# Storing each 1 MiB output tile as two 64-partition transfers in a pairwise-product kernel

## The chip, the cores and the metric

The kernel runs on one core of a Trainium2 chip. The metric is the device time of one execution in microseconds (us). Before the change it is 766.14 us, the median of three runs that lie between 765.97 and 767.21 us. The profiled execution has a span of 769.8 us, from its first to its last instruction.

## What is computed

The inputs are 1024 samples of 32 fields, each a vector of 128 numbers, and one 128x128 matrix for each of the 496 pairs of fields (i, j) with i < j. Everything is float32.

```python
v_i = inputs[:, I_IDX, :]                        # 1024 x 496 x 128
v_j = inputs[:, J_IDX, :]
transformed = jnp.einsum('bpd,ped->bpe', v_i, W) # one 128x128 matrix per pair
return transformed * v_j                         # 1024 x 496 x 128
```

The output is 1024 x 496 x 128 float32 numbers, 260 MB. The two inputs together are some 49 MB.

## The kernel before

**Layout.** The 128 embedding entries lie on the 128 partitions. A field is a tile `x_f` of 128 partitions x 1024 samples, and all 32 fields stay resident after their load. The host transposes the inputs before and the output after; in device memory the output is laid out as `(248, 128, 2, 1024)`: for each group of two pairs, 128 rows of 2 x 1024 numbers. So one row of one group is 8192 contiguous bytes, and one group is a contiguous block of 1 MiB.

**Loops.** The main loop goes over units `u`: unit `2q + h` is pair `q` and half `h` of the samples (512 of them, `HB`). `first(u)` does the matmuls for a unit into a PSUM tile `po` (L154 for the first 15 pairs in plain float32; L157 for the other pairs, with a matrix split in two parts, and L158 scales the result on ScalarE). `second(u)`, three units later (`LAG`), adds a third matmul (L166) and multiplies the result by field `j` on VectorE (L172), writing into the output tile `ot`. An `ot` tile holds one group, that is two pairs of 1024 samples on 128 partitions (1 MiB), and is filled by four multiplications. The pool has four `ot` tiles, so a fifth group can be started only when the store of the first has landed. ScalarE (L94, L109) and GpSimd (L95 to L97, L110 to L115) split matrices and fields into high and low parts ahead of their use; VectorE does some of the last subtractions (L195).

**Transfers.** The matrices come in 124 blocks of four pairs, a load of 256 KiB each (L85), 16 pairs ahead; the fields come in loads of 512 KiB (L76), five fields ahead. The group's store is issued when its fourth multiplication is queued (L176). All stores and, but for the four first field loads, all loads are issued from the same queue, that of SyncE (SP), in the order of the program[...]. The last group is stored in four pieces (L174), one for each half of each pair. Each transfer raises one of eight semaphores, taken in turn.

Of the kernel before, what the change touches and what calls it, by code (L numbers as in the profile page):

```python
# [1 line left out]

# [4 lines left out]

F32 = mybir.dt.float32
F32R = mybir.dt.float32r
ALU = mybir.AluOpType  # L10

P = 128
NF = 32
NQ = NF * (NF - 1) // 2
BT = 1024
HB = 512
WC = 2
WL = 4
OG = 2
EPS = 2.0**-12  # L20
NATIVE = 5
SHARED = 10
XDLAG = 10
LAG = 3
WLEAD = 4
XLEAD = 5


def _pairs():

    return [(i, j) for i in range(NF - 2, -1, -1) for j in range(i + 1, NF)]


@with_exitstack
def kernel(
    ctx: ExitStack,
    tc: tile.TileContext,
    xt: bass.AP,
    wt: bass.AP,
    out: bass.AP,  # L40
):

    nc = tc.nc
    pairs = _pairs()
    nchunk = NQ // WC  # L60

    xpool = ctx.enter_context(tc.tile_pool(name="x", bufs=1))
    spool = ctx.enter_context(tc.tile_pool(name="xs", bufs=2))
    rpool = ctx.enter_context(tc.tile_pool(name="wr", bufs=5))
    wpool = ctx.enter_context(tc.tile_pool(name="ws", bufs=4))
    opool = ctx.enter_context(tc.tile_pool(name="o", bufs=4))
    ppool = ctx.enter_context(tc.tile_pool(name="ps", bufs=8, space=bass.MemoryType.PSUM))

    x_sb = {}

    def load_x(f, n=1, pieces=1, eng=None):

        t = xpool.tile([P, n, BT], F32, tag=f"x{f}", name=f"x_{f}")
        s = BT // pieces
        for k in range(pieces):
            (eng or nc.sync).dma_start(out=t[:, :, k * s : (k + 1) * s], in_=xt[:, f : f + n, k * s : (k + 1) * s])  # L76
        for k in range(n):
            x_sb[f + k] = t[:, k, :]

    w_raw = {}  # L80

    def load_w(c, splits=(0, WL)):
        w_raw[c] = rpool.tile([P, WL, P], F32, tag="w", name=f"w_{c}")
        for a, b in zip(splits, splits[1:]):
            nc.sync.dma_start(out=w_raw[c][:, a:b, :], in_=wt[c, :, a:b, :])  # L85

    w_s = {}

    def split_w(c, u):

        k = c * WC % WL
        raw = w_raw[c * WC // WL][:, k : k + WC, :].rearrange("p q e -> p (q e)")
        h, l, d = [wpool.tile([P, WC * P], F32R, tag=t, name=f"{t}_{c}") for t in ("wh", "wl", "wd")]
        nc.scalar.mul(h, raw, 1.0 - 2.0**-13)  # L94
        nc.gpsimd.tensor_tensor(l, raw, h.bitcast(F32), ALU.subtract)  # L95
        nc.gpsimd.tensor_scalar(d, h.bitcast(F32), EPS, 1.0, ALU.mult, ALU.mult)  # L96
        nc.gpsimd.tensor_tensor(d, l.bitcast(F32), d.bitcast(F32), ALU.subtract)  # L97
        w_s[c] = (h, l, d)

    x_s = {}  # L100
    later = []

    def split_x(f, a, u):

        if a == 0:
            x_s[f] = [spool.tile([P, BT], F32R, tag=t, name=f"{t}_{f}") for t in ("xh", "xl", "xd")]
        s = slice(a, a + HB)
        h, l, d = [t[:, s] for t in x_s[f]]
        nc.scalar.mul(h, x_sb[f][:, s], 1.0 - 2.0**-13)  # L109
        nc.gpsimd.tensor_tensor(l, x_sb[f][:, s], h.bitcast(F32), ALU.subtract)  # L110
        nc.gpsimd.tensor_scalar(l, l.bitcast(F32), 1.0 / EPS, 1.0, ALU.mult, ALU.mult)  # L111
        if f > NF - 2 - NATIVE - SHARED:
            later.append((min(u + XDLAG, 2 * first_q[f] + LAG - 1), d, h.bitcast(F32), l.bitcast(F32)))
        else:
            nc.gpsimd.tensor_tensor(d, h.bitcast(F32), l.bitcast(F32), ALU.subtract)  # L115

    nq0 = NATIVE * (NATIVE + 1) // 2
    c0 = nq0 // WC
    first_q = {i: q for q, (i, j) in reversed(list(enumerate(pairs)))}

    todo = []
    for c in range(c0, nchunk):
        todo.append(((c - 3) * WC + 1, max(c * WC, nq0), lambda u, c=c: split_w(c, u)))
    for i in range(NF - 2 - NATIVE, -1, -1):
        for a in range(0, BT, HB):
            todo.append((first_q[i + 1] + 1 if i < NF - 3 - NATIVE else 2, first_q[i], lambda u, i=i, a=a: split_x(i, a, u)))
    todo.sort(key=lambda t: t[1])

    load_w(0, (0, 1, WL))
    load_x(NF - 2, pieces=2, eng=nc.scalar)
    load_x(NF - 1, pieces=2, eng=nc.scalar)
    load_x(NF - 3)
    load_x(NF - 4)
    load_w(1)
    for f in range(NF - 5, NF - 4 - XLEAD, -1):
        load_x(f)
    load_w(2)
    load_w(3)  # L140


    ctx.enter_context(tc.manual_schedule())
    po, ots = {}, {}


    def first(u):
        q, h = divmod(u, 2)
        i, c = pairs[q][0], q // WC
        r = slice(q % WC * P, (q % WC + 1) * P)  # L150
        s = slice(h * HB, (h + 1) * HB)
        po[u] = ppool.tile([P, HB], F32, tag="po", name=f"po_{u}")
        if q < nq0:
            nc.tensor.matmul(po[u], w_raw[q // WL][:, q % WL, :], x_sb[i][:, s], start=True, stop=True)  # L154
        else:
            for t in (0, 1):
                nc.tensor.matmul(po[u], w_s[c][t][:, r], x_s[i][t][:, s], start=t == 0, stop=t == 1)  # L157
            nc.scalar.mul(po[u], po[u], 1.0 + EPS)  # L158

    def second(u):  # L160
        q, h = divmod(u, 2)
        i, j = pairs[q]
        r = slice(q % WC * P, (q % WC + 1) * P)
        s = slice(h * HB, (h + 1) * HB)
        if q >= nq0:
            nc.tensor.matmul(  # L166
                po[u], w_s[q // WC][2][:, r], x_s[i][2][:, s], start=False, stop=True, skip_group_check=True
            )
        g, k = divmod(q, OG)
        if k == 0 and h == 0:  # L170
            ots[g] = opool.tile([P, OG, BT], F32, tag="ot", name=f"ot_{g}")
        nc.vector.tensor_tensor(ots[g][:, k, s], po.pop(u), x_sb[j][:, s], ALU.mult)  # L172
        if q >= NQ - 2:
            nc.sync.dma_start(out=out[g, :, k, s], in_=ots[g][:, k, s])  # L174
        elif k == OG - 1 and h == 1:
            nc.sync.dma_start(out=out[g], in_=ots[g])  # L176

    for u in range(2 * NQ + LAG):
        q = u // 2
        if u % (2 * WL) == 0 and (q // WL + WLEAD) * WL < NQ:  # L180
            load_w(q // WL + WLEAD)
        if u < 2 * NQ:
            i, j = pairs[q]
            if u % 2 == 0 and j == i + 1 and 0 <= i - 2 - XLEAD:
                load_x(i - 2 - XLEAD)
            first(u)
        if u >= LAG:
            second(u - LAG)
        if u % 2 == 1:
            ready = [t for t in todo if t[0] <= q]  # L190
            if ready:
                ready[0][2](u)
                todo.remove(ready[0])
        while later and later[0][0] <= u:
            nc.vector.tensor_tensor(*later.pop(0)[1:], ALU.subtract)  # L195
    assert not todo and not later


# [25 lines left out]
```

## Time and profile before

| what | value |
|---|---|
| time, median of 3 runs | 766.14 us (765.97 to 767.21) |
| span of the profiled execution | 769.8 us |
| busy: TensorE matmul, VectorE, ScalarE, GpSimd | 722.7, 632.0, 638.7, 593.2 us |
| bytes moved by the DMA engines | 310.11 MB, mean 403 GB/s |
| written to device memory, read from it | 260.05 MB, 49.28 MB |
| granted TensorE clock | 0.994 of full speed |

The bytes and their rate say what the 16 DMA engines of the core did over the whole span. The busy time of a compute engine is a sum over its instructions; an engine may be busy all the time and still not set the end, so the chain of waits has to be read beside it.

### The profile page before, as it was taken

How to read it: one execution, taken by the hardware profiler on the slowest of the kernel's cores; microseconds unless marked ns; L12 is line 12 of the kernel's file. 1: busy time of each engine (PE TensorE's matmuls, PEld its weight loads, DVE VectorE, ACT ScalarE, POOL GpSimd, SP SyncE). 2: the span in 40 equal slices, each digit the busy share in tenths (PEclk: the TensorE clock that was granted, in tenths of full speed). 3: DMA queues.
4: the chain of work that ended last, by engine and by line, in shares of the span. 5: the costliest groups of instructions: out<-in, count | busy, mean ns of one | idle time of the engine just before them, and what ended most of it. 6: DMA issues, size and time to landing. Idle time of an engine off the chain costs nothing.

```text
span 769.8 us, 11824 instructions
## 1 busy us (share of the span) xinstructions
PE 722.7 (94%) x2946; PEld 545.4 (71%) x2946; DVE 632.0 (82%) x1012; ACT 638.7 (83%) x1256; POOL 593.2 (77%) x863
## 2 busy tenths in 40 slices
PE   7988999999999999999999989999999999999994
PEld 3556766677777676777777767777777777777773
DVE  4869888888888788888888878888888888888885
ACT  2276988888888898888888889998988898998983
POOL 2677998887889878878878696978786969697660
PEclk9999999999999999999999999999999999999998
DMA  9999999999999999999999999999999999999997
GB/s 352 424 419 384 407 397 410 405 400 406 410 405 403 400 409 416 409 379 421 411 414 407 412 403 406 411 407 408 415 410 395 408 410 409 409 408 405 400 401 307
DMA packets 59108, 310.11 MB, mean 403 GB/s; under 512 B 6560, under 2 KB 6816, under 8 KB 27424
## 3 DMA queue, kind: packets, MB, share of 16 engines
q1 hardware_dynamic: 58464, 308.31, 99.4%
q10 hardware_dynamic: 576, 1.05, 0.4%
q8 instruction: 24, 0.39, 0.2%
q14 instruction: 44, 0.36, 0.1%
HBM read 49.28 MB, written 260.05 MB: 402 GB/s over the span
## 4 chain that ended last, share of the span: by engine, by line
DMA 61%; DVE 21%; PE 15%; issue 2%; DVEq 0%; SPq 0%; ACT 0%
DMA out_dram<-ot 60%; DVE ot L172 19%; PE po L157 9%; PE po L166 4%; DVE xd L195 2%; PE po L154 1%; DMA x<-in_xt_dram 1%; DVEq L172 0%; SPq L85 0%; DVEq L217 0%; ACT po L158 0%; DVEq L195 0%
## 5 line engine op out<-in xcount | busy, mean ns | idle before, releaser
L172 DVE TENSOR_TENSOR ot<-po,x 128x512 f32<-128x512 f32 x992 | 618.6, 684 | 129.5 <-DMA out_dram<-ot 70.2
L158 ACT ACTIVATE po<-po 128x512 f32<-128x512 f32 x962 | 551.2, 583 | 106.5 <-PE po L157 53.3
L157 PE MATMUL po<-xh,wh 128*128 128x512 f32 x962 | 388.7, 404 | 24.4 <-DVE ot L172 21.6
L166 PE MATMUL po<-xd,wd 128*128 128x512 f32 x962 | 376.9, 392 | 5.7 <-DVE xd L195 5.7
L157 PE MATMUL po<-xl,wl 128*128 128x512 f32 x962 | 377.6, 392 | 2.2 <-POOL wl L95 2.1
L157 PEld LDWEIGHTS po<-xh,wh 128*128 128x128 f32 x962 | 180.9, 188 | 110.2 <-DVE ot L172 72.5
L95 POOL TENSOR_TENSOR wl<-w,wh 128x256 fp32r<-128x256 f32 x241 | 179.2, 744 | 92.1 <-ACT wh L94 90.7
L166 PEld LDWEIGHTS po<-xd,wd 128*128 128x128 f32 x962 | 181.0, 188 | 46.3 <-ACT po L158 3.8
L157 PEld LDWEIGHTS po<-xl,wl 128*128 128x128 f32 x962 | 181.1, 188 | 36.8 <-POOL wl L95 4.5
L97 POOL TENSOR_TENSOR wd<-wl,wd 128x256 fp32r<-128x256 f32 x241 | 180.0, 747 | 20.1
L96 POOL TENSOR_SCALAR wd<-wh 128x256 fp32r<-128x256 f32 x241 | 99.1, 411 | 20.3
L94 ACT ACTIVATE wh<-w 128x256 fp32r<-128x256 f32 x241 | 99.2, 412 | 0.5 <-DMA w<-in_wt_dram 0.5
L110 POOL TENSOR_TENSOR xl<-x,xh 128x512 fp32r<-128x512 f32 x52 | 67.3, 1293 | 19.8 <-ACT xh L109 19.5
L115 POOL TENSOR_TENSOR xd<-xh,xl 128x512 fp32r<-128x512 f32 x32 | 41.4, 1292 | 2.7
L109 ACT ACTIVATE xh<-x 128x512 fp32r<-128x512 f32 x52 | 32.5, 628 | 10.5 <-DMA x<-in_xt_dram 10.3
L111 POOL TENSOR_SCALAR xl<-xl 128x512 fp32r<-128x512 f32 x52 | 32.8, 631 | 4.6
L154 PE MATMUL po<-x,w 128*128 128x512 f32 x60 | 29.0, 645 | 4.1 <-DMA x<-in_xt_dram 4.1
L154 PEld LDWEIGHTS po<-x,w 128*128 128x128 f32 x60 | 12.1, 206 | 20.2 <-issue 13.9
L195 DVE TENSOR_TENSOR xd<-xh,xl 128x512 fp32r<-128x512 f32 x20 | 16.6, 831 | 0.0
L109 ACT ACT_TABLE_LOAD x1 | 1.3, 1283 | 2.6 <-issue 2.6
L211 POOL MEMSET const-float32-0.0<- 128x1 f32 x1 | 0.1, 98 | 0.2 <-issue 0.2
L211 POOL MEMSET const-bfloat16-1.0<- 128x1 bf16 x1 | 0.1, 101 | 0.0
(2 smaller groups left out, 0.2 us busy)
## 6 DMA issues: line engine op xcount, KB each, us to landing
out_dram<-ot SPq DMA_DIRECT2D x247, 1024.0 KB, 8.9
w<-in_wt_dram SPq DMA_DIRECT2D x123, 256.0 KB, 9.1
x<-in_xt_dram SPq DMA_DIRECT2D x30, 512.0 KB, 9.5
x<-in_xt_dram ACTq DMA_DIRECT2D x4, 256.0 KB, 5.1
out_dram<-ot SPq DMA_DIRECT2D x4, 256.0 KB, 7.0
w<-in_wt_dram SPq DMA_DIRECT2D x1, 192.0 KB, 3.6
w<-in_wt_dram SPq DMA_DIRECT2D x1, 64.0 KB, 2.9
```

The source lines that it names most:

```text
L94: nc.scalar.mul(h, raw, 1.0 - 2.0**-13)
L95: nc.gpsimd.tensor_tensor(l, raw, h.bitcast(F32), ALU.subtract)
L96: nc.gpsimd.tensor_scalar(d, h.bitcast(F32), EPS, 1.0, ALU.mult, ALU.mult)
L97: nc.gpsimd.tensor_tensor(d, l.bitcast(F32), d.bitcast(F32), ALU.subtract)
L109: nc.scalar.mul(h, x_sb[f][:, s], 1.0 - 2.0**-13)
L110: nc.gpsimd.tensor_tensor(l, x_sb[f][:, s], h.bitcast(F32), ALU.subtract)
L115: nc.gpsimd.tensor_tensor(d, h.bitcast(F32), l.bitcast(F32), ALU.subtract)
L154: nc.tensor.matmul(po[u], w_raw[q // WL][:, q % WL, :], x_sb[i][:, s], start=True, stop=True)
L157: nc.tensor.matmul(po[u], w_s[c][t][:, r], x_s[i][t][:, s], start=t == 0, stop=t == 1)
L158: nc.scalar.mul(po[u], po[u], 1.0 + EPS)
L166: nc.tensor.matmul(po[u], w_s[q // WC][2][:, r], x_s[i][2][:, s], start=False, stop=True, skip_group_check=True)
L172: nc.vector.tensor_tensor(ots[g][:, k, s], po.pop(u), x_sb[j][:, s], ALU.mult)
```

## The change

The store of a group, one transfer of 128 partitions, becomes two transfers of 64 partitions each, issued one behind the other from the same queue: first partitions 0 to 63, then 64 to 127. The bytes, their place in memory, the length of the rows (8192 bytes) and the condition for issuing (the group's four multiplications) stay as they are. It is for changing which partitions each of the 16 DMA engines reads: a transfer's rows are shared out among the engines[...]. The four small stores of the last group are not touched.

```diff
         elif k == OG - 1 and h == 1:
-            nc.sync.dma_start(out=out[g], in_=ots[g])
+            for a in range(0, P, P // 2):
+                nc.sync.dma_start(out=out[g, a : a + P // 2], in_=ots[g][a : a + P // 2])
```

## Prediction

> **What bounds the kernel now.** I read the page's slices and DMA part first, since the kernel writes 260 MB; then the chain that ended last; then one stretch of it in order of time; then the waits of the issuing queue. The page:
>
> ```profile
> DMA  9999999999999999999999999999999999999997
> DMA packets 59108, 310.11 MB, mean 403 GB/s; under 512 B 6560, under 2 KB 6816, under 8 KB 27424
> q1 hardware_dynamic: 58464, 308.31, 99.4%
> HBM read 49.28 MB, written 260.05 MB: 402 GB/s over the span
> DMA 61%; DVE 21%; PE 15%; issue 2%; DVEq 0%; SPq 0%; ACT 0%
> out_dram<-ot SPq DMA_DIRECT2D x247, 1024.0 KB, 8.9
> w<-in_wt_dram SPq DMA_DIRECT2D x123, 256.0 KB, 9.1
> ```
>
> The 16 DMA engines have packets in every slice, and one queue's packets fill 99.4% of what 16 engines have. A store takes 8.9 us from issue to landing, and a load a quarter of its size takes 9.1 us: neither moves for that long, both stand in line. The busy time by stretches says the same for the steady part:
>
> ```profile
> core 0: us, PE busy (x) PEld busy (x) DVE busy (x) ACT busy (x) POOL busy (x), PEclk, DMA share, GB/s
> 540.00:640.00 100.00, 98.40 (x413) 75.96 (x412) 85.46 (x138) 90.69 (x179) 78.80 (x117) 1.00 1.01 407
> ```
>
> DMA share 1.01 at 407 GB/s: the engines never rest, 407 / 16 = 25.4 GB/s each. TensorE shows 98% too, but the chain decides:
>
> ```profile
> 23 pieces in order of time: start us, us, what
> 635.72 8.91 DMA out_dram<-ot
> ...
> 644.76 2.50 DVE ot L172 x4
> ...
> 647.27 8.98 DMA out_dram<-ot
> ...
> 656.37 2.50 DVE ot L172 x4
> ...
> 658.88 8.93 DMA out_dram<-ot
> ```
>
> The chain is a ring: a store lands, VectorE fills the freed tile (2.50 us), its store lands 8.9 us later. One turn is 647.27 - 635.72 = 11.55 us and covers four groups, as there are four `ot` tiles: 2.89 us a group. In a turn the queue moves four stores (4.19 MB) and two matrix loads (0.52 MB), 4.72 MB / 11.55 us = 408 GB/s, the rate above. So the ring's period is the DMA engines' throughput; the 8.9 us is queueing behind other stores. By bytes, a store has 11.55 x 4 / 4.5 / 4 = 2.57 us of it, a matrix load 0.64 us.
>
> The issuing queue has room:
>
> ```profile
> SPq L176 <- DVE ot L172: 481.8, 244, 4.4
> ```
>
> (who waits for whom on it: us in total, times, longest), and by the tile's view
>
> ```profile
> L176 SPq DMA_DIRECT2D out_dram<-ot x247: 332/332/1258, 14.3 to 759.0; - x124
> ```
>
> It stands 481.8 us waiting for VectorE; an issue costs 332 ns.
>
> [...] Here each of the 128-partition transfers raises its semaphore by 16 single steps. [...]
>
> **The change part by part.**
>
> Descriptors: each of 247 stores has a second completion write on each engine. The trace's packet records give 9 ns for one: 247 x 0.009 = 2.2 us, on the path, as the engines never rest.
>
> Issue: 247 more issues of 332 ns are 82 us of the queue, beside its 481.8 us of waiting: hidden. Behind the second issue stands at most a matrix or field load, 0.33 us later; loads run 16 pairs ahead (eight groups, 23 us), so nobody waits. Eight semaphores taken in turn may make an issue wait for the eighth transfer before it. Per group there are now 2 halves + 0.5 load = 2.5 transfers (1.5 before), so eight are 3.2 groups; today 8.9 / 2.89 = 3.1 groups are in flight. The engines keep about the same amount queued: 0.
>
> Engine work: the same 64 KiB per engine and store. If each engine still gave 25.4 GB/s, nothing else would change.
>
> Ports: this is the term that counts. Each engine takes four rows (32 KiB) of the lower half, then four of the upper. [...] By half of today's 407 GB/s it takes 5.15 us, +2.57. [...]
>
> They are not fully in step. [...] From the semaphore steps in the trace: of the 16 engines of a transfer, twelve finish within 0.69 us (median), the others 1.9 to 4.7 us after the first. Two of the twelve are thus some 0.3 us apart (my choice within 0 to 0.69), while a half takes 2.57 / 2 = 1.29 us. Sharing then holds for (1.29 - 0.3) / 1.29 = 77%[...].
>
> The compute engines, faster than this, wait: VectorE's four multiplications (4 x 0.68 = 2.7 us a group) lie within 4 us or more of storing.
>
> **The rivals.**
>
> *Ports do not bind, or the engines fall into opposite halves.* [...] Also, the trace before cannot tell whether 25.4 GB/s is the engine's or the port's limit. Then only the completion writes count: 766.1 + 2.2 = 768.3 us, slower by 0.3%. [...]
>
> *Slow packets vanish (faster).* The mean packet is 11 ns over the median; if the new sharing-out spreads the addresses so that all are gone, 8 x 247 x 0.011 = 22 us is saved, less 2.2: 746 us. If a quarter goes, 763 us. For it: the chain is DMA throughput, so it would count in full. Against it: nothing ties the slow packets to partitions[...].
>
> *The queue's semaphores become the wait.* If issues waited for older transfers so that only two groups were in flight, the ring would be two groups in about 2.5 (fill) + 5.8 us (two groups' transfers of 2.89), 4.1 us a group, near 1030 us. Worked out above, 3.2 groups stay possible; I give it little.
>
> **How the numbers follow.** Ports shared, mostly in step to half in step (about 940 to 1340 us): 0.74. Ports shared but engines well apart, or the semaphore wait alone (770 to 940): 0.05. No port effect, completion writes only (around 768): 0.08, half of it within 0.2%. Faster: 0.13. So faster 0.13, within 0.2% 0.04, slower 0.83. The predicted time is that of the likeliest case, 1190 us. The upper end takes in [...]some of the 5.15 us price: 1340. The first case alone holds less than 8 in 10, so the lower end reaches down to the completion-write case, 768 us.
>
> **What would show it.** Right: the share of the DMA engines stays near 1 while GB/s falls to about 260 (310 MB / 1.19 ms); 8192-byte packets go from 309 ns to some 500 to 610; a half's time to landing exceeds 8.9 us clearly; TensorE and VectorE fall to about 60 and 53% busy with the same busy time per instruction; the chain goes nearly all to the DMA; VectorE's wait for the store, 70.2 us in total now, grows to several hundred. Wrong: packets still at 309 ns and 400 GB/s, which means that the ports do not bind; or packets at 309 ns with gaps between them (DMA share below 0.9), which means a wait for issue or semaphores. [...]

## The result and the profile after

The changed kernel takes 1034.24 us (median of four runs, 1027.89 to 1039.99) against 766.67 us (four runs, 765.97 to 773.16), 1.347 times the time before, with a 95% interval of 1.339 to 1.356. The profiled execution has a span of 1033.4 us.

The page of the changed kernel: DMA totals, the main queue, the chain by engine, VectorE's multiplications (busy, mean ns | idle before, releaser) and the median us from issue to landing.

```profile
DMA packets 63064, 310.16 MB, mean 300 GB/s; under 512 B 10512, under 2 KB 10768, under 8 KB 31376
q1 hardware_dynamic: 62416, 308.32, 94.7%
DMA 67%; DVE 18%; PE 7%; SPq 4%; issue 2%; DVEq 1%; POOL 0%; ACT 0%; POOLq 0%
L172 DVE TENSOR_TENSOR ot<-po,x 128x512 f32<-128x512 f32 x992 | 619.8, 684 | 388.6 <-DMA out_dram<-ot 312.9
out_dram<-ot SPq DMA_DIRECT2D x494, 512.0 KB, 6.6
w<-in_wt_dram SPq DMA_DIRECT2D x123, 256.0 KB, 5.8
```

The bytes are the same to 0.05 MB, the rate falls from 403 to 300 GB/s, and the packet count grows by 247 x 16 = 3952 packets of 4 bytes, the completion writes (6561 before, 10513 after, 8.9 ns each), and four packets of other queues. A multiplication still takes 684 ns; VectorE now waits 312.9 us for stores (70.2 before). So the loss lies in the transfers. But a half lands in 6.6 us (a whole store before: 8.9) and a load in 5.8 (9.1): the line in front of each transfer is shorter than before, not longer. The stretch shown before, again:

```profile
core 0: us, PE busy (x) PEld busy (x) DVE busy (x) ACT busy (x) POOL busy (x), PEclk, DMA share, GB/s
540.00:640.00 100.00, 73.83 (x288) 53.15 (x287) 59.55 (x96) 64.62 (x125) 56.81 (x84) 0.98 0.95 294
```

The engines are at work for 0.95 of the time (1.01 before) and move 294 GB/s (407): their packets have become slower, and some 5% of the time they have none. Both can be read from the packet records. Per engine (sums over all packets, divided by 16), packets took 770.4 us before and 984.3 us after: 8192-byte ones +184.2 us (mean 320 to 413 ns), 2048-byte ones +18.7, 4096-byte ones +8.7, completion writes +2.3. The span is longer than their sum by 1033.4 - 984.3 = 49.1 us, by nothing before. 184.2 + 18.7 + 8.7 + 2.3 + 49.1 = 263 us is the whole difference of the two spans, 263.6 us.

Where the second part comes from shows in the issuing queue. The timeline of SyncE, the kernel before first (start us, us, then what; xN joins N neighbours):

```profile
start us, us, engine line op out<-in xcount [idle before <-releaser]
606.78 2.91 SPq L176 DMA_DIRECT2D out_dram<-ot  x2
609.79 0.73 SPq L85 DMA_DIRECT2D w<-in_wt_dram  x1
612.61 2.88 SPq L176 DMA_DIRECT2D out_dram<-ot  x2
615.58 0.79 SPq L85 DMA_DIRECT2D w<-in_wt_dram  x1
```

and the changed kernel:

```profile
start us, us, engine line op out<-in xcount [idle before <-releaser]
605.84 6.08 SPq L177 DMA_DIRECT2D out_dram<-ot  x4
612.02 1.53 SPq L85 DMA_DIRECT2D w<-in_wt_dram  x1
613.64 6.52 SPq L177 DMA_DIRECT2D out_dram<-ot  x4
620.25 1.54 SPq L85 DMA_DIRECT2D w<-in_wt_dram  x1
```

The pieces before have pauses within them: two issues of 0.33 us in 2.9 us. After, four issues fill 6.1 to 6.5 us without one. The output tile's view gives one issue (ns, min/median/max), before it was 332/332/1258:

```profile
L177 SPq DMA_DIRECT2D out_dram<-ot x494: 466/1631/2746, 14.0 to 1023.6; - x165
```

This price isn't all due to the form of the transfer. An issue that began less than 0.15 us after the end of the one in front of it was long before the change too. There these were mostly the matrix loads, whose issues stand right behind a store's. They too are transfers of 128 partitions; the view of their tile, before the change:

```profile
L85 SPq DMA_DIRECT2D w<-in_wt_dram x125: 327/1002/1694, 0.7 to 731.8; - x125
```

After the first 60 us, the median of all issues that stood right behind another was 1047 ns before the change (128 issues) and 1646 ns after it (598). Issues that came after a pause of over 1 us took 332 ns before; after the change there is no such pause left.

After the first 60 us SyncE's queue is inside an issue for 95% of the time (31% before), and in the stretch shown a group's first store starts to issue 4.5 to 6.3 us after the group's last multiplication (0.03 us before). The chain of the changed kernel shows it only faintly:

```profile
607.27 5.68 DMA out_dram<-ot
...
613.08 1.90 DVE ot L172 x3
614.97 0.42 SPq L177
...
615.45 5.75 DMA out_dram<-ot
```

One should not read this as "fill, then a short issue": the multiplications here are those of a later group than the store that follows. With four tiles the true ring is fill, about 5 us in line for the queue, two issues, about 5 us to land.

### The profile page after: what moved, and what is told of

Read it like the earlier page. It is cut to its first block, busy times and chain, and to the rows that moved or that the text cites. A ratio compares the mean times of both kernels' runs of the same rounds, so it can differ in the third digit from the quotient of the medians.

```text
span 1033.4 us, 12309 instructions
## 1 busy us (share of the span) xinstructions
PE 775.9 (75%) x2946; PEld 552.6 (53%) x2946; DVE 634.1 (61%) x1012; ACT 655.2 (63%) x1256; POOL 592.3 (57%) x863
## 4 chain that ended last, share of the span: by engine, by line
DMA 67%; DVE 18%; PE 7%; SPq 4%; issue 2%; DVEq 1%; POOL 0%; ACT 0%; POOLq 0%
DMA out_dram<-ot 65%; DVE ot L172 17%; PE po L157 5%; SPq L177 4%; PE po L166 2%; DMA x<-in_xt_dram 1%; DVE xd L196 1%; DVEq L172 1%; POOL wd L97 0%; POOL wl L95 0%; POOL wd L96 0%; SPq L85 0%; ACT po L158 0%; DVEq L218 0%; ACT wh L94 0%
## 5 line engine op out<-in xcount | busy, mean ns | idle before, releaser
L172 DVE TENSOR_TENSOR ot<-po,x 128x512 f32<-128x512 f32 x992 | 619.8, 684 | 388.6 <-DMA out_dram<-ot 312.9
L157 PE MATMUL po<-xh,wh 128*128 128x512 f32 x962 | 410.8, 427 | 227.9 <-DVE ot L172 227.3
L166 PE MATMUL po<-xd,wd 128*128 128x512 f32 x962 | 386.8, 402 | 10.3 <-DVE xd L196 10.3
L157 PE MATMUL po<-xl,wl 128*128 128x512 f32 x962 | 387.1, 402 | 0.0
L157 PEld LDWEIGHTS po<-xh,wh 128*128 128x128 f32 x962 | 185.8, 193 | 361.7 <-DVE ot L172 322.7
L95 POOL TENSOR_TENSOR wl<-w,wh 128x256 fp32r<-128x256 f32 x241 | 177.0, 734 | 327.1 <-ACT wh L94 325.7
L166 PEld LDWEIGHTS po<-xd,wd 128*128 128x128 f32 x962 | 186.4, 194 | 55.0 <-issue 9.2
L157 PEld LDWEIGHTS po<-xl,wl 128*128 128x128 f32 x962 | 187.0, 194 | 29.0 <-issue 0.2
```

The lines of the kernel that those rows point to most:

```text
L166: nc.tensor.matmul(po[u], w_s[q // WC][2][:, r], x_s[i][2][:, s], start=False, stop=True, skip_group_check=True)
```

## The experiments

Two theories stood against each other: **ports**, as the expectations call it, by which DMA engines slow each other down while they read the same half of the partitions; and **issue**, a queue that became the limit because there are more transfers. What engines would share in a half, no trace or run of this case shows; the runs test whether reading one half at the same time costs time. The *lead theory* adds that engines whose positions in the queue are apart slow each other down for a smaller part of the stretch that they spend in one half. It too is a theory to be tested. A time without an interval is that of a single run; four runs of the changed kernel lie within 1.2% of each other. All diffs are against the changed kernel, except where another is named.

**The same number of transfers, cut by pair.**

```diff
-            for a in range(0, P, P // 2):
-                nc.sync.dma_start(out=out[g, a : a + P // 2], in_=ots[g][a : a + P // 2])
+            for a in range(OG):
+                nc.sync.dma_start(out=out[g, :, a], in_=ots[g][:, a])
```

> Each group's store is cut in two by pair instead of by partition: two transfers of 128 partitions x 4096 bytes. As many transfers as in the changed kernel[...]. Ports theory[...]: no sharing, so near the kernel before; the rows are half as long, 4096-byte packets take 159 ns where half an 8192-byte one takes 154.5, so 8 x 247 x 9 ns = 18 us more: about 785 us. Issue theory (SyncE's queue, whose issues took 1.6 us each in the changed kernel, is the limit because there are more transfers): about 1030 us again, with issues of about 1.6 us.

779.68 us, 1.017 times before (1.015 to 1.019). One issue, from the tile's view:

```profile
L177 SPq DMA_DIRECT2D out_dram<-ot x494: 332/333/1799, 14.0 to 766.6; - x165
```

494 transfers of 128 partitions cost 13 us, most of it their shorter packets (162 ns against half of 320: 16 x 247 x 2 ns = 8 us) and 2 us of completion writes. The count of transfers alone doesn't make the loss. On issues the run says less than it seems to: the first transfer of a group now waits for its own pair only and starts 1.2 us before the group's last multiplication ends, so that most issues follow a pause. Those right behind another took 1095 ns (median of 135), as before the change.

**Both halves from the lower partitions.**

```diff
-                nc.sync.dma_start(out=out[g, a : a + P // 2], in_=ots[g][a : a + P // 2])
+                nc.sync.dma_start(out=out[g, a : a + P // 2], in_=ots[g][0 : P // 2])
```

> Both transfers of a group read partitions 0 to 63 of the output tile (so rows 64 to 127 of the output receive the lower half's numbers). Count and shape of the transfers are those of the changed kernel[...]. Ports theory: [...]about 1320 us, packets near 610 ns. Issue theory: 1030 us as before, packets unchanged.

1305.9 us, the number of the first theory, and it fixes the price of full sharing (all stores read one half) at 1306 - 766 = 540 us. By stretches:

```profile
540.00:640.00 100.00, 72.50 (x231) 51.59 (x230) 47.55 (x77) 52.45 (x100) 48.33 (x70) 0.83 0.99 240
```

The engines are busy for 0.99 of the time and move 240 GB/s, loads included, 15 GB/s each (25.4 before). The packet records have most 8192-byte packets between 590 and 650 ns, mean 574, median 627: about twice the 309 ns of before.

**Even partitions, then odd ones.**

```diff
-            for a in range(0, P, P // 2):
-                nc.sync.dma_start(out=out[g, a : a + P // 2], in_=ots[g][a : a + P // 2])
+            for a in range(2):
+                nc.sync.dma_start(out=out[g, a::2], in_=ots[g][a::2])
```

> Two transfers of 64 partitions again, but the even partitions and then the odd ones[...]. Ports theory:[...]between 770 and 1000 us. Issue theory: 1030 us again.

773.0 us in one run, 0.8% above before. 64 rows of 8192 bytes and 494 transfers as in the changed kernel, but each transfer spread over all partitions: packets are back at a mean of 317 ns, and an issue at 614 ns (998 ns for the 405 right behind another, although here, as in the changed kernel, both transfers wait for the group's four multiplications):

```profile
L177 SPq DMA_DIRECT2D out_dram<-ot x494: 471/614/2128, 13.6 to 760.9; - x165
```

and by stretches the engines are as busy and as fast as before the change:

```profile
540.00:640.00 100.00, 97.20 (x408) 74.86 (x406) 83.82 (x136) 89.48 (x177) 78.42 (x115) 1.00 1.01 403
```

It isn't the number of partitions in a transfer that costs, but which ones. One rival isn't excluded: even and odd rows also land elsewhere in device memory than halves, each of which is a contiguous 512 KiB. The lower-half run writes to the same places as the changed kernel, in the same order, and takes 272 us longer, so the partitions that are read do count. But no run kept the places of the halves and filled them from all partitions.

**Turned order in every second group.**

```diff
-            for a in range(0, P, P // 2):
+            for a in ((0, P // 2), (P // 2, 0))[g % 2]:
```

> The changed kernel with the two halves of every second group issued in turned order: lower, upper, upper, lower, so that an engine reads eight rows in the same half in a row instead of four. Same transfers, same number. Lead theory[...]: the stretch doubles to 2.6 us, the same leads of about 0.6 us count half as much, about 75% of the time shared instead of 50%: 766 + 0.75 x 540 = about 1170 us, between the changed kernel and the one that reads the lower half alone (1306). Rival (the share of sharing doesn't depend on leads, or the issue queue sets the time): 1034 us as before.

1150.7 us, mean packet 465 ns.

```profile
540.00:640.00 100.00, 66.23 (x260) 47.78 (x261) 54.65 (x88) 57.87 (x111) 50.33 (x75) 0.99 0.95 268
```

The same transfers in another order cost 116 us more. Together: stretches of four rows in one half cost 268 us, of eight rows 384, without end 540. A count of transfers doesn't explain that; the lead theory had given about 1170 us beforehand. The leads themselves were measured in no run, as the packet records don't name the engine.

**Matrix loads in halves, stores whole** (against the kernel before).

```diff
-            nc.sync.dma_start(out=w_raw[c][:, a:b, :], in_=wt[c, :, a:b, :])
+            for p in range(0, P, P // 2):
+                nc.sync.dma_start(out=w_raw[c][p : p + P // 2, a:b, :], in_=wt[c, p : p + P // 2, a:b, :])
```

> The kernel before (whole stores), with each matrix load in two transfers of 64 partitions: sharing in the direction into the chip's memory, in stretches of four 2048-byte rows, 0.34 us. In step, a load would take 1.34 us instead of 0.67, 124 x 0.67 = 83 us more: 850 us. By the lead theory, leads of 0.3 us and more end nearly all sharing of so short a stretch: 767 to 785 us, of which 124 x 9 ns = 1 us are completion writes.

783.22 us, 1.019 times before (1.013 to 1.024), within what the lead theory gave. About half of the 14 us is lost at the start, where the first two of the page's 40 slices (19.5 us each) move 275 and 346 GB/s instead of 352 and 424: 3.0 MB, or 7 us at 407 GB/s. The loads' packets are hardly slower over the whole run (87 ns against 86), and yet their issues are long:

```profile
L86 SPq DMA_DIRECT2D w<-in_wt_dram x250: 465/1334/2047, 0.7 to 743.8; - x125
```

Right behind another, an issue took 1356 ns here (median of 358), against 1047 in the kernel before. So most of this length is that of any issue right behind another, and some 0.3 us go with 64 neighbouring partitions even where packets aren't slow.

**The upper half from ScalarE's queue.**

```diff
-            for a in range(0, P, P // 2):
-                nc.sync.dma_start(out=out[g, a : a + P // 2], in_=ots[g][a : a + P // 2])
+            for a, eng in ((0, nc.sync), (P // 2, nc.scalar)):
+                eng.dma_start(out=out[g, a : a + P // 2], in_=ots[g][a : a + P // 2])
```

> The 64-partition halves as in the changed kernel, but the upper one is issued from ScalarE's queue. Issue theory: SyncE issues 1.5 transfers a group instead of 2.5, 1.5 x 1.6 = 2.4 us, under the 2.9 us of a group before: back to about 770 to 800 us. Ports theory: [...]unless the two queues happen to put engines in opposite halves; 1000 us or so if they do not, below 900 us if they do, with packets near 309 ns.

950.3 us, neither number. Packets stay slow (mean 403 ns) with the engines at 0.99, so they remain the larger part; but 84 us came back. Two things changed at once, the load on SyncE's queue and the order in which engines meet the halves, so this run doesn't say which. The next three separate more of it.

**All loads from ScalarE's queue.**

```diff
-            nc.sync.dma_start(out=w_raw[c][:, a:b, :], in_=wt[c, :, a:b, :])
+            nc.scalar.dma_start(out=w_raw[c][:, a:b, :], in_=wt[c, :, a:b, :])
 ...
-            (eng or nc.sync).dma_start(...)
+            (eng or nc.scalar).dma_start(...)
```

> The changed kernel with the matrix and field loads issued from ScalarE's queue; SyncE issues the halves alone, two transfers a group instead of 2.6. If the long issues of SyncE (1.6 us each, queue busy 95%) set the pace, a group costs 2 x 1.63 = 3.3 us instead of 4.1: about 850 us. If the issues are long only because the engines behind take no more, the time stays within 40 us of 1034 and the issues get longer, to about 2 us each.

928.9 us, between the two expectations: 105 us less than the changed kernel. Its stretch,

```profile
540.00:640.00 100.00, 84.23 (x346) 62.98 (x345) 70.92 (x116) 76.32 (x149) 68.27 (x102) 1.00 0.99 335
```

and one issue, from the tile's view:

```profile
L177 SPq DMA_DIRECT2D out_dram<-ot x494: 466/1647/2989, 14.8 to 917.0; - x165
```

The stores' issues are as long as before the move (1647 ns against 1631). The engines' share is back at 0.99, and packets also are faster (mean 386 ns): per engine 912.3 us of packets and 14.9 us without, against 984.3 and 49.1. Two controls belong to it, with the same edit. On the kernel before (whole stores):

> The control of the run with the loads on ScalarE's queue: the kernel before (whole stores on SyncE's queue), all loads issued by ScalarE. If moving the loads does something of its own, it shows here. Both theories: nothing is bound by issue or ports here, so 766 us within 1%; then the 105 us that the move saved with halved stores belong to the halves.

766.28 us, 0.998 times before (0.997 to 0.9995): the move does little or nothing by itself. The loads' issues, with nothing right in front of them now, are short:

```profile
L85 ACTq DMA_DIRECT2D w<-in_wt_dram x125: 334/334/877, 0.7 to 725.2; - x125
```

And on the kernel that reads the lower half twice:

> Both transfers of a group from partitions 0 to 63 (rows 64 to 127 of the output receive the lower half's numbers), and the loads on ScalarE's queue. Where all engines share all the time, [...]the long issues only mirror it: about 1300 us again (1306 with the loads on SyncE's queue). If the issues were the bound there too, two a group of 2.1 us instead of 2.6: about 1050 us.

1308.7 us (1305.9 without the move).

```profile
540.00:640.00 100.00, 72.19 (x230) 51.59 (x229) 47.71 (x77) 52.18 (x100) 48.01 (x69) 0.84 0.99 234
```

Where all stores read one half, the time is the same within 3 us, whichever queue the loads come from. So the 105 us appear where the stores read both halves, and not where they read one. Whether they come from the shorter line of issues on SyncE's queue or from the other order in which engines meet loads and halves, the three runs don't tell.

## Why the prediction was right, and where its sizes were off

**The direction and the term that counts: right, and shown.** A store that all engines read from one half of the partitions takes about twice as long: its packets go from 309 to 627 ns (medians). By half of the 407 GB/s of before, a store costs 2.57 us more, 635 us for all 247; the kernel that reads one half alone took 1306 us, 540 us more. The 1190 us rested on a lower price than 635 us, which no trace of before shows. The completion writes were put at 2.2 us and measured at 2.3. The trace before could not tell whether one half could feed all 16 engines at 25.4 GB/s each; the lower-half run shows that it doesn't (240 GB/s, 15 each). What limits a half, and which engines would share it, no run shows.

**The lead: mis-sized.** "Sharing then holds for (1.29 - 0.3) / 1.29 = 77%": of the 540 us measured for full sharing, that would be 416 us, where the change cost 1034 - 767 = 268, 50%. The 0.3 us was a choice, taken from twelve engines of the kernel before; the others, up to 4.7 us behind, were set aside. In the changed kernel twelve of the 16 completions of a half lie within 1.16 us in place of 0.69, and all 16 within 1.68 us in place of 4.7 (medians after the first 60 us). So leads of 0.6 us and more are plausible, but which engines slow each other down isn't known, and their leads weren't measured. By packets alone the sharing is smaller still: (413 - 320) / (574 - 320) = 37% of the slowdown of the lower-half run. The rest up to 50% is mainly the 49 us in which engines had nothing to do, a term that the prediction had put at 0.

**The issues: wrong.** "247 more issues of 332 ns are 82 us of the queue, beside its 481.8 us of waiting: hidden." An issue took 1631 ns, not 332, and the queue was occupied for 95% of the time. Three to four transfers are under way after an issue, where the eight semaphores would allow eight; the engines ran short (49 us), and a half landed in 6.6 us where I had expected clearly more than 8.9. I had taken the issue's price from the nearest row, a store that came after a pause; the row of the matrix loads, which stand right behind a store, had 1002 ns. Even at that price the issues would have been hidden (247 more are some 250 us, beside 481.8 us of waiting); the rest of the 1631 ns stood in no trace of before. The rival that named a wait on the issuing queue blamed the semaphores; the time in issue itself was missing from it. That its number, near 1030 us, lies so close to the result is chance: it left the packets at their old speed, and the semaphores were not the limit. What the issues cost isn't measured by itself. The loads' move, which took about a quarter of them from the queue, brought back 105 us of 268, of which 34 us are engine time without packets and 72 us faster packets.

**Why fewer issues make packets faster is argued, not shown.** The start of the changed kernel fits the idea that a short line brings engines back into step. By stretches:

```profile
28.00:40.00 12.00, 10.84 (x38) 6.53 (x38) 8.59 (x14) 6.40 (x13) 6.21 (x11) 1.00 1.03 386
42.00:60.00 18.00, 13.86 (x50) 9.93 (x49) 9.94 (x16) 11.84 (x24) 11.22 (x16) 0.91 0.93 314
```

From 28 to 40 us data moved at nearly the full rate, 386 GB/s, and the 8192-byte packets took 335 ns in the mean, hardly more than before the change (311 ns), which suggests that engines were mostly in opposite halves; no record shows it. Between 20 and 40 us the transfers under way went down from eight to about three, as most issues took 1.4 to 2.0 us. From 42 us on the rate is 314 GB/s and packets take 381 ns; later the rate is about 300. The alternative, that loads on a queue of their own change the engines' order, isn't excluded: no run lengthened the line while leaving that order alone.

**The other signs.** VectorE's wait for stores went to 312.9 us ("several hundred": right); TensorE and VectorE fell to 75 and 61% busy (60 and 53 expected, in keeping with the longer forecast; TensorE's busy time also grew from 722.7 to 775.9 us); the DMA engines' share fell to 0.95 and the rate to 300 GB/s, where a share near 1 and 260 GB/s were expected; the chain is 67% DMA (61 before), where nearly all of it was expected; 8192-byte packets are split between about the old 309 ns, for half of them, and up to some 650 ns, rather than all at 500 to 610. The rival "slow packets vanish" is out: the run with as many rows in a transfer and no sharing to be seen (even and odd partitions, 773.0 us) isn't faster than before.

## What to carry to other kernels

When the transfers are the bound, look at which partitions are read at the same time, not only at bytes and rows: transfers of 64 rows cost 0.8% when they were spread over all partitions, and 35% as contiguous halves. For transfers of half the partitions, try orders with shorter stretches in one half: with four rows in a row this kernel took 1034 us, with eight 1151, the same transfers in another order. And an issue's duration isn't one number: here it was 332 ns after a pause and 1047 ns right behind another issue before the change, and 1646 ns right behind another after it. Take its price from issues that stand as the new ones will, and read it again after the change, before counting the queue as free.

## What was not expected of the hardware

- A transfer of 128 partitions is issued in 332 ns after a pause, and in about 1.0 to 1.1 us right behind another issue (medians 1047 ns in the kernel before, 1095 cut by pair). Even and odd partitions: 472 and 998 ns.
- Where 64 neighbouring partitions are stored or loaded, issues right behind another are longer still: 1356 ns with split loads, 1646 in the changed kernel, 2037 in turned order, 2160 with the lower half twice. The order is that of the slow packets (means of 8192-byte ones: 322, 413, 465, 574 ns), so the length may in part mirror them; but the run with halves and all loads moved falls out of it (1702 ns, 386 ns), and with split loads packets weren't slow. What makes it long stays open.
- Engines fed half by half kept nearly the full rate for 12 us (386 GB/s) early in the kernel, then lost it (314 GB/s). That they were in opposite halves is inferred from the fast packets (335 ns, then 381).
- With twice as many stores of 128 partitions (cut by pair), seven to eight transfers were under way, and a quarter of the issues began some 0.06 us or less after the eighth one before had landed: the eight semaphores were at their limit, and yet the run is only 1.7% longer.
